# A two-layer transformer block with experts and a state-space scan: scatters that don't wait for each other, and scan inputs made in another order

## The chip, the cores and the metric

The kernel runs on one core of one Trainium2 chip. The metric is device time in microseconds (us), as the median of repeated executions. A core has five engines with their own instruction streams: TensorE (PE in the profile; its weight loads are PEld), VectorE (DVE), ScalarE (ACT), GpSimd (POOL) and SyncE (SP, which here only issues DMAs). They wait for each other by semaphores. TensorE writes to PSUM, a small memory in banks of 128 x 512 float32; all other data lie in SBUF or in the chip's main memory.

## What is computed

Four sequences (B = 4) of 1024 tokens with 128 features pass two layers. Each layer modulates a layer norm by shift and scale, adds a gated mixer, norms again and adds a gated mixture of experts. The mixer of layer 0 is causal attention with 16 heads; that of layer 1 is a selective scan. Cut to what matters:

```python
# layer 0
h = _layernorm(x) * (1 + ca) + sa
x = x + ga * attention(h)                       # 16 heads, causal
h = _layernorm(x) * (1 + cb) + sb
x = x + gb * ffn0(h)     # 8 experts, each token goes to its best 2
# layer 1
x_conv = silu(conv1d(x_main) + conv_b)          # x_main, z = split(h @ W_in)
B_sel, C_sel, delta = ..., ..., softplus(x_conv @ W_xproj[:, -1])
h_t = exp(delta_t * A) * h_(t-1) + delta_t * B_t * u_t      # the scan
y_t = sum_n h_t * C_t
y = (y + x_conv * D_param) * silu(z);  x = x + ga * (y @ W_out)
# then 8 experts again, top 2, with a capacity of tokens for each expert
```

Tokens are sorted to experts by their router's choice. On the chip this is a scatter: each token's normed row (128 float32) is written to a table in main memory at its expert's place, the experts read blocks of rows from the table, write their results to another table, and a gather brings them back.

## The kernel before

**Attention (0 to about 1402 us).** Eight stages, one for each sequence and half of the heads, each with eight blocks of 128 queries in the order 7, 0, 6, 1, 5, 2, 4, 3. A block's scores come from TensorE (`sc`), VectorE adds the mask and finds the maximum (L644), ScalarE exponentiates (L657), POOL divides by the sum (`pr`, L663), TensorE turns the result (`pt`, L672) and multiplies by the values (`po`). POOL also clears a part of the next `pr` (memset, L793) and adds results to `x` (L191).

Beside it, in the stages (1,0), (2,0) and (3,0), runs the **sorting** of the sequence before it (`sort_tokens`, from L364): norm, router, top 2, places, and then 16 scatters (L418), one for each tile of 128 tokens and each choice. The experts of that sequence (`Blocks`) run in the following stage; their first step reads the table (`fxe`, L440).

**The scan stage (1404 to 1848 us).** `scan_inputs(b)` (L923) makes, for one sequence: norm `xn`, turned features `hT`, convolution `p1` and its activation `xc`, `z`'s activation `sz`, `delta` (`pd`, softplus, `dg`), `dt`, `du` = dt*xc (L977, POOL), `bb` and `cc`. Every matmul of it writes to one PSUM bank, tag "m" (bufs = 1), except for sequence 0. `scan` (L988) then runs 32 chunks for each sequence: a product `pu` (TensorE), its multiplication by `bb` (L997, VectorE), `da` (L999, ScalarE), the scan `h` (L1001, VectorE), and `hc` = h*cc (L1005, POOL). `py` collects four `hc` on TensorE, and `scan_output` finishes half a sequence.

The main loop (from L1275) goes over the sequences and, after each pair of chunks, takes a few steps of generators that run beside the scan (`Beside`: from which pair on, how many steps): the inputs of the next sequence, the sort of sequence 3 and its experts, the returns, and the **dispatch** of the sequence before it (L1027: norm, router, places and 16 scatters `slots_in`, L1088, to two tables in turn, one for each choice). The Tile framework schedules the issued instructions onto the engines' queues by its own priorities; every engine then works its queue in order. A scatter is an indirect DMA that POOL issues; a second one into the same table is taken for a write to the same place and waits until the first has landed.

**After the scan.** The last dispatch, the experts of layer 1, eight for each of two choices (1884 to 2006 us), the last half sequence's own table (`g_in`, eight scatters), and the returns.

Of the kernel before, what the change touches and what calls it, by code (L numbers as in the profile page):

```python
# [18 lines left out]
P = 128  # L19
# [30 lines left out]
def adaln_two_layers(ctx: ExitStack, tc: tile.TileContext, I: dict, out: bass.AP):  # L50
# [14 lines left out]
    def load(pool, name, eng=nc.sync):  # L65
# [9 lines left out]

    causal = cst.tile([P, P], F32, name="causal")
    nc.gpsimd.memset(causal, 0.0)
    nc.gpsimd.affine_select(
        out=causal, in_=causal, compare_op=ALU.is_ge, fill=NEG, base=0, pattern=[[-1, P]], channel_multiplier=1
    )  # L80
# [251 lines left out]
    kept, first_made = {}, []  # L332
# [31 lines left out]
    def sort_tokens(b, kept, pool, ps, hpool, tag, xtag="fxn"):  # L364
# [5 lines left out]
        yield from feature_steps(xn, hT, ps, modT[0][:, 4, b : b + 1], modT[0][:, 3, b : b + 1])  # L370
        pl = ps.tile([P, TB, NE], F32, tag="m", name="fpl")
# [8 lines left out]
        pin = ps.tile([P, TB + 1, NE], F32, tag="m", name="fpin")  # L380
        pinf = pin.rearrange("p t e -> p (t e)")
        mm(nc, pinf[:, : TB * NE], before, flat, stop=False)
        for n in range(1, TB):
# [3 lines left out]
        mm(nc, pin[:, TB, :], ones, mine)  # L387
        yield
# [8 lines left out]
        blocks, upto, which = yield from find_blocks(pin[:, TB, :], NB, sm)  # L397
# [7 lines left out]
            pos, upto.unsqueeze(1).to_broadcast([P, TB, NE]), float(P), pin[:, :TB, :], ALU.mult, ALU.add  # L405
# [9 lines left out]
        kept[b] = expert, placei, w  # L415
        for t in range(TB):
            for k in range(2):
                nc.gpsimd.indirect_dma_start(  # L418
                    out=f_in[b][:, :],
                    out_offset=bass.IndirectOffsetOnAxis(ap=placei[:, k, t : t + 1], axis=0),  # L420
                    in_=xn[:, t, :],
                    in_offset=None,
                )
                yield

    class Blocks:
# [9 lines left out]
        def load(self, n):  # L436
            rows_in = f_in[self.b].rearrange("(q p) d -> p q d", p=P)
            m = min(3, NB - 3 * n)
            self.xe = self.pool.tile([P, 3, D], F32, tag="fxe", name="fxe")
            nc.sync.dma_start(self.xe[:, :m], rows_in[:, 3 * n : 3 * n + m])  # L440
# [55 lines left out]
    with ExitStack() as es:  # L496
# [23 lines left out]
        MW = 512 + QG  # L520
        mask = aw.tile([P, MW], F32, name="mask")
# [5 lines left out]
        def zero_steps():  # L527

            for slots in f_in + xd + [g_in]:
                flat = slots.rearrange("(p r) d -> p (r d)", p=P)  # L530
                for at in range(0, flat.shape[1], 512):
                    n = min(512, flat.shape[1] - at)
                    nc.sync.dma_start(flat[:, at : at + n], mask[:, :n])
                    yield
# [234 lines left out]
        zeros, gates = zero_steps(), gate_steps()  # L769
        for at, (b, c) in enumerate(stages):  # L770
# [9 lines left out]
            for n, i in enumerate(order):  # L780
# [13 lines left out]
                for g in range(4):  # L794
# [14 lines left out]
                    if at < 2:  # L809
                        next(zeros, None)  # L810
# [8 lines left out]
            if at == 1:  # L819
                drained(zeros)  # L820
# [32 lines left out]
    with ExitStack() as es:  # L853
# [69 lines left out]
        def scan_inputs(b):  # L923

            def made_of(g, to, w, of):
                bank = ps_m.tile([P, 512], F32, tag=next(tags), name="p1")
                mm(nc, bank, w, of)
                nc.scalar.copy(to[:, half_of(g)], bank)
# [10 lines left out]
            if b == 0:  # L939
                xc, sz, dl = first_made  # L940
                tags = itertools.cycle(("m", "d"))
                dg = spread_delta(dl)

                for g in range(2):
                    tok = half_of(g)
                    made_of(g, dt, ones, dg[g])
                    nc.gpsimd.tensor_mul(du[:, tok], dt[:, tok], xc[:, tok])
                    made_of(g, bb, m_B, xc[:, tok])
                    made_of(g, cc, m_C, xc[:, tok])
                return sz, xc, dt, du, bb, cc  # L950
            tags = itertools.repeat("m")
# [10 lines left out]
            for g in range(2):  # L962
                tok = half_of(g)
                p1 = ps_m.tile([P, 512], F32, tag="m", name="p1")
# [3 lines left out]
                p2 = ps_m.tile([P, 512], F32, tag="m", name="p2")  # L968
                mm(nc, p2, m_in[:, D:], hT[:, tok.start + 3 : tok.stop + 3])
                nc.scalar.activation(sz[:, tok], p2, AF.Silu)  # L970
                yield
            dl = yield from delta_steps(xc, ps_m)
            dg = spread_delta(dl)
            yield
            for g in range(2):
                made_of(g, dt, ones, dg[g])
            nc.gpsimd.tensor_mul(du, dt, xc)  # L977
            yield

            for to, w in ((bb, m_B), (cc, m_C)):  # L980
                for g in range(2):
                    made_of(g, to, w, xc[:, half_of(g)])
                yield
# [118 lines left out]
        def dispatch_last():  # L1102
# [63 lines left out]
            for t in range(nt):  # L1166
                for k in range(2):
                    nc.gpsimd.indirect_dma_start(
                        out=g_in[:, :],
                        out_offset=bass.IndirectOffsetOnAxis(ap=placei[:, k, t : t + 1], axis=0),  # L1170
                        in_=hx[:, t, :],
                        in_offset=None,
                    )
# [7 lines left out]
        sent = []  # L1181

        def last_experts():
# [11 lines left out]
            def rows(q):  # L1195
                n = min(4, nb - q)
                ins[q] = eb.tile([P, 4, D], F32, tag="gxe", name="gxe")
                nc.sync.dma_start(ins[q][:, :n], rows_in[:, q : q + n])
# [76 lines left out]
        for b in range(B):  # L1275
# [3 lines left out]
            if b == 0:  # L1279
                beside.append(Beside(first_returns(B - 2, db, 6), 4, 1))  # L1280
                beside.append(Beside(sort_tokens(B - 1, kept, db, ps_m, db, "hT2", "hx"), 2, 4))
# [7 lines left out]
            if b + 1 < B:  # L1289
                inputs = Beside(scan_inputs(b + 1), 5 if b == 2 else 2, 3 if b == 2 else 2)  # L1290
                beside.append(inputs)
            hcs, late = [], None
# [230 lines left out]
```

## Time and profile before

| what | value |
|---|---|
| three runs | 2079.97, 2082.40 and 2082.79 us; median 2082.4 |
| the profiled execution | 2072.22 us, its span 2070.5 |
| mean granted TensorE clock | 0.923 of full speed |
| attention | 0 to about 1402 us |
| scans, first to last | 1415 to 1848.5 us |
| experts of layer 1 | 1884 to 2006 us |
| a scan `h`, 128 x 512 | 1209 ns, with a carry 1268 (medians) |
| a scatter `blocks_in` on POOL | 982 ns (median of 64), landing 2.3 us after issue |

The page gives each engine's busy time, the span in 40 slices, the groups of instructions by line, and the releasers of idle time. Busy shares over the span hide the stages. So the trace is read by stretches: the busy time of each engine between two moments, beside the granted clock (PEclk). A waits row names who waited, for whom, the total, how often, and the longest. A timeline row has the start, the duration, the engine and line, and in brackets the idle time before it and what ended that.

### The profile page before, as it was taken

How to read it: one execution, taken by the hardware profiler on the slowest of the kernel's cores; microseconds unless marked ns; L12 is line 12 of the kernel's file. 1: busy time of each engine (PE TensorE's matmuls, PEld its weight loads, DVE VectorE, ACT ScalarE, POOL GpSimd, SP SyncE). 2: the span in 40 equal slices, each digit the busy share in tenths (PEclk: the TensorE clock that was granted, in tenths of full speed). 3: DMA queues.
4: the chain of work that ended last, by engine and by line, in shares of the span. 5: the costliest groups of instructions: out<-in, count | busy, mean ns of one | idle time of the engine just before them, and what ended most of it. 6: DMA issues, size and time to landing. Idle time of an engine off the chain costs nothing. (4 is left out here: it accounts for less than half of the span.)

```text
span 2070.5 us, 29042 instructions
## 1 busy us (share of the span) xinstructions
PE 1779.8 (86%) x8957; PEld 964.2 (47%) x8957; DVE 1331.4 (64%) x4005; ACT 944.8 (46%) x2071; POOL 1000.4 (48%) x1282
## 2 busy tenths in 40 slices
PE   5999899898999899899989899997779757757994
PEld 2444454453555345455535445553335423325774
DVE  5666556665667666566766566567858887782144
ACT  2364453743455374355455445455556345422321
POOL 3345335446333634633363653227654775773145
PEclk8899999999999999999999999998879887967997
DMA  6502002002222201212210122111003230002255
GB/s 202 186 1 52 1 1 52 1 26 63 64 64 78 56 1 32 78 54 71 78 40 1 48 68 68 51 43 38 31 27 111 76 108 13 8 20 83 80 156 177
DMA packets 104332, 124.63 MB, mean 60 GB/s; under 512 B 15088, under 2 KB 68720, under 8 KB 104176
## 3 DMA queue, kind: packets, MB, share of 16 engines
q1 hardware_dynamic: 83872, 98.75, 15.9%
q0 software_dynamic: 8192, 16.74, 2.7%
q10 hardware_dynamic: 12112, 7.29, 1.2%
q8 instruction: 71, 1.16, 0.2%
q14 instruction: 85, 0.70, 0.1%
HBM read 68.38 MB, written 33.42 MB: 49 GB/s over the span
## 5 line engine op out<-in xcount | busy, mean ns | idle before, releaser
L663 POOL TENSOR_SCALAR pr<-pr,den 128x32 f32<-128x32 f32 (+31 forms) x512 | 356.2, 711 | 308.2 <-DVE den L660 300.2
L657 ACT ACTIVATE pr<-pr,nb 128x32 f32<-128x32 f32 (+31 forms) x512 | 371.7, 727 | 164.5 <-DVE nb L644 158.5
L672 PE MATMUL pt<-ident,pr 128*128 128x128 f32 x2304 | 342.2, 283 | 47.2 <-POOL pr L663 37.2
L672 PEld LDWEIGHTS pt<-ident,pr 128*128 128x128 f32 x2304 | 253.9, 142 | 242.5 <-POOL pr L663 78.1
L46 PE MATMUL sc<-k,q 64*128 64x512 f32 (+14 forms) x1536 | 333.6, 527 | 33.6 <-DVE nb L644 25.5
L46 PE MATMUL po<-pT,v 128*64 128x512 f32 x1152 | 342.6, 621 | 2.8 <-DVE pT L676 2.8
L674 ACT COPY pT<-pt 128x512 f32<-128x512 f32 x288 | 167.5, 582 | 353.9 <-PE pt L672 302.5
L644 DVE CUSTOM_DVE_ANT_0 pr<-sc,mask 128x512 f32<-128x512 f32 (+15 forms) x512 | 272.8, 559 | 67.4 <-PE sc L46 57.0
L676 DVE COPY pT<-pt 128x512 f32<-128x512 f32 x288 | 198.2, 688 | 159.4 <-PE pt L672 145.9
L46 PEld LDWEIGHTS sc<-k,q 64*128 64x128 f32 x1536 | 125.4, 195 | 186.9 <-DVE nb L644 88.6
L1005 POOL TENSOR_TENSOR hc<-h,cc 128x512 f32<-128x512 f32 x128 | 161.7, 1276 | 87.7 <-DVE h L1001 32.2
L46 PE MATMUL pu<-du,spread 128*128 128x512 f32 x256 | 149.6, 694 | 54.5 <-DVE h L1001 43.5
L793 POOL MEMSET pr<- 128x288 f32 x128 | 42.4, 340 | 245.8 <-PE pt L672 241.6
L644 DVE CUSTOM_DVE_ANT_0 pr<-sc,mask,nb 128x416 f32<-128x416 f32 (+15 forms) x256 | 120.0, 496 | 7.3 <-PE sc L46 6.2
L999 ACT ACTIVATE da<-dt,negA 128x512 f32<-128x512 f32 x128 | 91.4, 718 | 62.7 <-DVE h L1001 62.3
L46 PEld LDWEIGHTS po<-pT,v 128*64 128x64 f32 x1152 | 68.9, 135 | 84.0 <-issue 41.4
L46 PEld LDWEIGHTS pu<-du,spread 128*128 128x128 f32 x256 | 47.6, 213 | 128.4 <-DVE h L1001 74.6
L1391 POOL DMA_INDIRECT y<-slots_out,slot x56 | 56.6, 1010 | 88.4 <-PE ph L46 52.1
L613 POOL TENSOR_TENSOR q<-rot_u,rot_v 128x512 f32<-128x512 f32 x64 | 81.3, 1272 | 36.4 <-DMA rot_v<-rot_w 35.3
L997 DVE TENSOR_TENSOR pu<-pu,bb 128x512 f32<-128x512 f32 x128 | 85.1, 684 | 18.0 <-PE pu L46 9.2
L657 ACT ACTIVATION_READ_ACCUMULATOR pr<-pr,nb 128x1 f32 x512 | 96.2, 188 | 0.0
L418 POOL DMA_INDIRECT blocks_in<-fxn,f_placei x64 | 64.6, 1009 | 57.3 <-DMA blocks_in<-fxn,f_placei 46.6
(281 smaller groups left out, 2695.3 us busy)
## 6 DMA issues: line engine op xcount, KB each, us to landing
fw<-in_f_w SPq DMA_DIRECT2D x92, 320.0 KB, 2.9
rot_v<-rot_w SPq DMA_DIRECT2D x300, 64.0 KB, 2.0
gw<-in_g_w SPq DMA_DIRECT2D x15, 512.0 KB, 5.7
fxe<-blocks_in SPq DMA_DIRECT2D x28, 192.0 KB, 2.5
blocks_out<-fye SPq DMA_DIRECT2D x28, 192.0 KB, 2.8
blocks_in<-mask SPq DMA_DIRECT2D x20, 256.0 KB, 2.9
slots_in<-mask SPq DMA_DIRECT2D x16, 256.0 KB, 3.7
g_w<-in_g_w SPq DMA_DIRECT2D x8, 512.0 KB, 7.3
```

The lines of the kernel that those rows point to most:

```text
L46: return nc.tensor.matmul(out, lhsT, rhs, start=start, stop=stop)
L418: nc.gpsimd.indirect_dma_start(out=f_in[b][:, :], out_offset=bass.IndirectOffsetOnAxis(ap=placei[:, k, t : t + 1], axis=0), in_=xn[:, t, : ...
L613: nc.gpsimd.tensor_add(to, u.rearrange("p (n q) -> p n q", q=QG), v.rearrange("p (n q) -> p n q", q=QG))
L644: nc.vector.tensor_tensor_reduce(out=pr[hp][:, g, lo:hi], in0=sc[:, hp, : hi - lo], in1=mask[:, MW - hi + lo :] if hi == nk else mask[:, : ...
L657: nc.scalar.activation(p, p, AF.Exp, bias=nb[:, last, hp : hp + 1], scale=-1.0, accum_out=den[:, hp : hp + 1])
L663: nc.gpsimd.tensor_scalar(p, p, den[:, hp : hp + 1], 1.0, ALU.mult, ALU.mult)
L672: next_to(hp == 0 and g == 0, lambda: nc.tensor.transpose(to, p, ident))
L674: nc.scalar.copy(pT[:, hp, :], pt)
L676: nc.vector.tensor_copy(pT[:, hp, :], pt)
L997: nc.vector.tensor_mul(pu, pu, bb[:, tok])
L999: nc.scalar.activation(da, dt[:, tok], AF.Exp, scale=negA[:, c : c + 1])
L1005: nc.gpsimd.tensor_mul(hcs[-1], h, cc[:, tok])
```

## The change

Four things, named by their place:

1. Scatters into one table no longer wait for each other. A new helper declares that they write different rows. A scatter now waits only for the clearing of its table, and a read of the table waits for all of its scatters. This holds for `blocks_in` (L418) and `g_in` (L1168), not for `slots_in`.
2. In sequence 0's loop, ten steps each are taken of the sort of sequence 3 and of `scan_inputs(1)`, ahead of the first scan.
3. `scan_inputs` for the sequences 1 to 3 makes `sz` after `delta`'s product, `bb` and `cc` between the steps of softplus, and `dt` and `du` last and in halves. Two PSUM banks take turns ("m" and "g"), except for sequence 2, which keeps one.
4. The sort of sequence 3 uses the PSUM bank "d"; the sort copies its counts from PSUM to SBUF (`ahead`) so that the bank comes free; the mask `causal` lies in a buffer of another pool.

```diff
+    def scatter(group, out, at, in_, fill):
+        ins = nc.gpsimd.indirect_dma_start(
+            out=out, out_offset=bass.IndirectOffsetOnAxis(ap=at, axis=0), in_=in_, in_offset=None
+        ).ins
+        if group:
+            tc.declare_no_dep(ins, group=group[0], reason="different rows")
+        else:
+            group.append(f"rows of {ins.name}")
+        tc.add_to_no_dep_group(group[0], ins)
+        after_all(ins, fill, "zeros")
+        group.append(ins)
+
+    def behind(read, group):
+        after_all(read.ins, group[1:], "scattered rows")
...
+        ahead = sm.tile([P, TB + 1, NE], F32, tag="f_ahead", bufs=1, name="f_ahead")
+        nc.vector.tensor_copy(ahead, pin)
...
-        nc.gpsimd.indirect_dma_start(
-            out=f_in[b][:, :],
...
+                scatter(arrived[b], f_in[b][:, :], placei[:, k, t : t + 1], xn[:, t, :], zeros[b])
...
-            nc.sync.dma_start(self.xe[:, :m], rows_in[:, 3 * n : 3 * n + m])
+            behind(nc.sync.dma_start(self.xe[:, :m], rows_in[:, 3 * n : 3 * n + m]), arrived[self.b])
...
-            tags = itertools.repeat("m")
+            free = b != 2
+            tags = itertools.cycle(((ps_m, "m"), (ps_g, "g"))) if free else itertools.repeat((ps_m, "m"))
...
-                p2 = ps_m.tile([P, 512], F32, tag="m", name="p2")
-                mm(nc, p2, m_in[:, D:], hT[:, tok.start + 3 : tok.stop + 3])
-                nc.scalar.activation(sz[:, tok], p2, AF.Silu)
                 yield
-            dl = yield from delta_steps(xc, ps_m)
-            dg = spread_delta(dl)
-            yield
+            delta = delta_steps(xc, ps_m)
+            next(delta)
             for g in range(2):
+                p2 = new_bank()
+                mm(nc, p2, m_in[:, D:], hT[:, g * 512 + 3 : g * 512 + 515])
+                nc.scalar.activation(sz[:, half_of(g)], p2, AF.Silu)
+            yield
+            try:
+                next(delta)
+                for g in range(2):
+                    made_of(g, bb, m_B, xc[:, half_of(g)])
+                yield
+                next(delta)
+                for g in range(2):
+                    made_of(g, cc, m_C, xc[:, half_of(g)])
+                yield
+                next(delta)
...
+            except StopIteration as end:
+                dg = spread_delta(end.value)
+            yield
+            for g in range(2):
+                tok = half_of(g)
                 made_of(g, dt, ones, dg[g])
-            nc.gpsimd.tensor_mul(du, dt, xc)
-            yield
-
-            for to, w in ((bb, m_B), (cc, m_C)):
-                for g in range(2):
-                    made_of(g, to, w, xc[:, half_of(g)])
-                yield
+                nc.gpsimd.tensor_mul(du[:, tok], dt[:, tok], xc[:, tok])
+            yield
...
-                beside.append(Beside(sort_tokens(B - 1, kept, db, ps_m, db, "hT2", "hx"), 2, 4))
+                beside.append(Beside(sort_tokens(B - 1, kept, db, ps_m, db, "hT2", "hx", "d"), 2, 4))
...
+            if b == 0:
+                for f in (beside[1], inputs):
+                    f.take(10)
```

## The prediction

> **What bounds the kernel now.** First the busy times: no engine is full over the whole span.
>
> ```profile
> PE 1779.8 (86%) x8957; PEld 964.2 (47%) x8957; DVE 1331.4 (64%) x4005; ACT 944.8 (46%) x2071; POOL 1000.4 (48%) x1282
> ```
>
> TensorE leads because attention (until about 1402 us) is its work; the change acts mostly where it does not lead. So the next view is busy time by stretch, cut at the first and last scans `h` of each batch:
>
> ```profile
> core 0: us, PE busy (x) PEld busy (x) DVE busy (x) ACT busy (x) POOL busy (x), PEclk, DMA share, GB/s
> 1415.10:1499.30 84.20, 65.80 (x200) 27.05 (x198) 73.45 (x133) 46.16 (x84) 58.17 (x54) 0.84 0.08 26
> 1499.30:1530.80 31.50, 17.69 (x46) 7.93 (x47) 9.39 (x57) 14.46 (x24) 15.04 (x15) 0.57 0.06 19
> 1530.80:1627.40 96.60, 84.91 (x414) 48.08 (x412) 86.81 (x181) 55.96 (x105) 50.87 (x45) 0.98 0.27 81
> 1627.40:1634.90 7.50, 6.11 (x17) 3.56 (x18) 1.95 (x7) 1.28 (x2) 6.84 (x7) 0.60 0.12 33
> 1634.90:1742.90 108.00, 75.81 (x288) 35.63 (x286) 92.23 (x184) 48.12 (x92) 76.18 (x64) 0.83 0.22 75
> 1742.90:1771.00 28.10, 17.40 (x70) 10.08 (x71) 10.90 (x53) 14.03 (x25) 21.70 (x19) 0.74 0.11 33
> 1771.00:1848.50 77.50, 54.60 (x164) 18.47 (x162) 73.87 (x116) 30.34 (x59) 57.54 (x48) 0.83 0.04 12
> 1848.50:1884.20 35.70, 13.18 (x52) 9.63 (x52) 21.49 (x85) 5.63 (x10) 20.09 (x19) 0.50 0.20 58
> ```
>
> Rows 1, 3, 5 and 7 are the four scan batches: VectorE is busy 85 to 95% of them and sets their length. Rows 2, 4 and 6 are stretches in which no scan runs: VectorE idles 22.1, 5.5 and 17.2 us there (length less its busy column). Those 44.8 us are what earlier inputs can win; the last row is the wait from the last scan to the experts.
>
> Third, what attention loses to scatters: POOL issues them, and each waits until the one before it has landed. The waits by engine have it (us in total, times, longest):
>
> ```profile
> POOL blocks_in L418 <- DMA blocks_in<-fxn,f_placei: 46.6, 35, 3.4
> ```
>
> 46.6 us of POOL waiting, 8.9 of it in the scan stage. Attention pays only where TensorE runs dry behind it; the timeline at 480 us is such a place:
>
> ```profile
> 481.74 0.98 POOL L418 DMA_INDIRECT blocks_in<-fxn,f_placei  x1 [3.20 <-DMA blocks_in<-fxn,f_placei]
> 484.26 0.97 POOL L418 DMA_INDIRECT blocks_in<-fxn,f_placei  x1 [1.54 <-DMA blocks_in<-fxn,f_placei]
> 485.25 1.27 POOL L608 TENSOR_TENSOR k<-rot_u,rot_v 128x512 f32<-128x512 f32 x1
> 486.49 1.52 POOL L663 TENSOR_SCALAR pr<-pr,den 128x608 f32<-128x608 f32 x2
> 487.31 0.18 PEld L672 LDWEIGHTS pt<-ident,pr 128*128 128x128 f32 x1 [7.68 <-POOL pr L663]
> ```
>
> Two chained scatters hold POOL, `pr` comes late, and TensorE starts its transposes 7.7 us late.
>
> **Part 1, unchained scatters in attention (three stages of 16).** Before, one takes 0.98 us plus 1.54 us of waiting, 2.5 us from start to start. The nearest row without a chain is `slots_in` (two tables in turn): starts at 1763.01, 1764.30 and 1765.59, 1.28 us. A table's 16 then hold POOL 20.5 us in place of some 40. But unchained they are also grouped otherwise: in the changed program's order on POOL they stand in runs of 2, 3, 1 and 10 in the first two stages, and 2, 5, 3, 1 and 5 in the third. A run of ten is 12.8 us; behind it on POOL wait the memset of the next `pr`, an add to `x`, and the normalisation of `pr`, for which TensorE waits. I followed the first stage: one `pr` comes 2.6 us later (TensorE loses some 2), the run of ten holds up a memset that VectorE's reduction needs (a new hole of about 3.5), and then POOL is free of scatters and the hole before 487.31 nearly goes (7.5 us, with what follows). Net gain 3 to 4 us; the second stage likewise 2 to 3; in the third a new 3 us stands against 4 us of idling at 1185 to 1189, net 2. I take **8 us of gain**. Ends: the three holes cost with their cold matmuls about 11, 9 and 13 us; losing 5 of them to nothing leaves 28 as the best; 5 us of loss, if the third hole stays in each stage beside the new one, less what TensorE catches up, is the worst I count.
>
> The change also adds waits: the tables' reads (`fxe`, on SyncE, with the weight loads `fw` queued behind) wait for all 16 scatters, and the scatters for the clearing of their table. The read waited for the last of the chain already, and the clearing ended stages earlier: 0, and if the last of the sixteen lands 2 us late, 2.
>
> The matmul clock weighs on this: it was granted at 0.50 from 484 to 492 us, behind the 7.5 us hole, but 1.00 between 1152 and 1155 us, in a 3.0 us hole, and 0.58 in the next 3. [...] The 64 scatters here beside busy VectorE took 966 to 1212 ns, median 982; the sum goes by these rows.
>
> **Part 2, inputs of batch 1 (gap of 31.5 us).** The chain there: last products of conv, `p`, `sz`, `pd` until 1511.9, softplus until 1518.4 shared with a norm, `dg` 1518.72, two matmuls of 2.06 with copies of 0.59 each (cold, clock 0.57), `du` in one piece from 1525.49 (2.35), `pu`, and
>
> ```profile
> 1530.08 0.70 DVE L997 TENSOR_TENSOR pu<-pu,bb 128x512 f32<-128x512 f32 x1 [8.59 <-ACT xn L168]
> ```
>
> The step that is late is the chain's start: the norm of batch 1 falls late in batch 0, its PSUM comes from one bank, and POOL alternates products `hc` with chained scatters (2.5 us each) until 1504. In the changed order the ten early steps of norm and features, two banks and free scatters put both halves of `du` behind `hc` 16 and 18 of 32, so the inputs are ready half a batch ahead. The gap's 9.4 us of VectorE work moves into batch 0, whose own idle is 10.8 us. Idle removed: 22.1 at best; I take **18**, because what is left of batch 0's chain (`hc`, `py`) must still end. Lower end 5, if batch 0 grows by most of it.
>
> **Part 3, what that costs at the head.** Two norms go ahead of the first scans' partners on ScalarE: 16 normalisations at 0.39 (five took 1.94) are 6.2 us, and three to four table loads of 1.28, part of which stand there already (1414 to 1422). Scans wait for `da` on ScalarE meanwhile. Total 6 to 11 us on ScalarE, covered by two or three scans in flight: I take **7 us of loss**, bounds 0 and 12.
>
> **Part 4, inputs of batches 2 and 3.** Halved `du` and the `dt` products: the first half's scan no longer waits for the second matmul and copy (2.1 + 0.6) and half of `du` (1.2): 3.9 us. Gap of 7.5: **3** (0 to 5.5). In the gap of 28.1 also the `du` at 1766.56 stood behind three scatters (1763.01 to 1766.56, 3.6 us), where now `slots_in` come earlier, between `hc` 88 and 96; and `sz` comes after `pd` (2 us). 3.9 + 3.6 + 2 = 9.5: **10** (4 to 17.2). What is late next is softplus, a chain of small VectorE operations.
>
> **Part 5, the tail.** Dispatch of batch 2, which used the last gap, now runs inside batch 3 and later: after the last `hc` stand 16 `slots_in` scatters where 8 stood. 8 × 1.28 = 10 us, partly beside the norm of the last rows: **6 us of loss** (0 to 10). The eight `g_in` scatters come back to back, but the first experts cover them: 0 (0 to 5 of gain). Four copies `f_ahead` of about 0.2 us: **1 of loss**. The mask `causal` in another buffer and the sort's own bank: 0; the sort's matmuls lie beside scans, and were the cover gone, a product waiting for bank "d" would cost about one 2 us step, which is inside the bounds.
>
> **Sum.** 8 + 18 − 7 + 3 + 10 − 6 − 1 = 25 us. The profiled execution took 2072.2 (span 2070.5 and 1.7 around it), so 2047 by its scale. It lies 10.2 below the median of the runs shown (2082.4); I forecast that median's successor, 2082.4 − 25 = **2057**. All good ends together would be 28 + 22 + 0 + 5.5 + 17 + 0 + 5 = 78, all bad ones −5 + 5 − 12 + 0 + 4 − 10 − 1 = −19; neither set is likely whole.
>
> **Rivals.**
> *Everything closes* (15%): attention's holes and all three gaps go, the tail stays covered. 28 + 22 − 7 + 5 + 14 − 6 = 56, so 2026. For it: VectorE's idle in the gaps is no work of any engine's own, the clock in the first gap is 0.57. Against: runs of ten on POOL.
> *VectorE and the tail take it back* (17%): batches 0 and 3 grow by most of what the gaps lose. Then 5 from part 2, 5 from part 4, 8 from attention, less 7 and 3: 8, so 2074. For it: VectorE is 95% busy in batch 3, so what moves there lengthens it.
> *It doesn't do what it says* (6%): the queue still takes one scatter of a table at a time, and 2.5 us stay from start to start. Then attention gives 0, part 2 its lower 5, part 4 3 and 4, less 7, 3 and 1: 1, so 2081, no measurable change. Against: two tables in turn did run at 1.28.
> *Slower, by runs of scatters on POOL* (12%). In attention TensorE stayed fed 3.3 us after its last `pr` (476.6 to 479.87). A run of ten holds POOL for 12.8, so 9.5 may be bare, and with 8 us at half clock as at 484 some 4 more: 13.5 in two stages, 3 in each of two runs of five in the third, 33 in all, if the old holes stay as well. With 17 left from the scan stage that is 16 slower, 2098. It decides where attention loses more than 17 us. Against: after the run POOL has no scatter left, and the old holes should go.
>
> **Numbers.** My own case, 2045 to 2069, 50%. Faster by over 0.2% (4 us, about what a measurement can tell from none): 50 + 15 + 17 = 82%; same 6%; slower 12%. The range 2024 to 2086 leaves out half of the first rival and the most of the last, some 17%.
>
> **What would show it.** Scatters of one table 1.28 us apart in all stages; no `pt` waiting 7 us for `pr` near 487, but a wait of about 3.5 for VectorE near 473 to 477; the next batch's first `h` within 10 us of the last at 1500, and 18 us in place of 28 before batch 3; batch 0 some 7 to 15 us longer; the tail about 41 us. It is wrong if batch 0 grows by over 20 us, or if attention ends later than before.

## The result, and the profile after

The changed kernel takes 2093.2 us (median of 5 runs, 2087.0 to 2095.8), the kernel before 2082.8 beside it (5 runs, 2080.0 to 2086.1): a ratio of 1.0041, 95% interval 1.0022 to 1.0060. It is slower by 0.2 to 0.6%, where 25 us of gain were forecast. A second measurement (e5 below) gave 1.0021 (1.0005 to 1.0037). A ratio here comes from runs made in turn, so the quotient of two medians can differ from it a little.

The profiled execution after has a span of 2085.2 us, clock 0.927. First the busy times from the page of the changed kernel:

```profile
PE 1776.4 (85%) x8957; PEld 959.8 (46%) x8957; DVE 1339.4 (64%) x4009; ACT 942.1 (45%) x2069; POOL 1002.8 (48%) x1285
```

Nearly nothing moves in them: VectorE has 8 us more with four instructions more. So again the stretches, cut at the first and last scan `h` of each batch (1.1 us lie between batches 0 and 1 now, and batches 1 and 2 touch):

```profile
core 0: us, PE busy (x) PEld busy (x) DVE busy (x) ACT busy (x) POOL busy (x), PEclk, DMA share, GB/s
1421.00:1527.30 106.30, 82.59 (x252) 36.07 (x250) 82.83 (x144) 53.36 (x98) 73.78 (x73) 0.81 0.10 31
1527.30:1528.40 1.10, 1.10 (x4) 0.56 (x4) 1.10 (x3) 0.72 (x1) 1.10 (x2) 1.00 0.00 0
1528.40:1649.30 120.90, 99.94 (x487) 59.20 (x486) 108.03 (x256) 63.46 (x123) 67.43 (x56) 0.93 0.29 84
1649.30:1753.50 104.20, 72.89 (x250) 29.75 (x248) 91.08 (x186) 50.33 (x92) 75.47 (x65) 0.83 0.16 59
1753.50:1767.80 14.30, 7.99 (x21) 3.27 (x22) 4.02 (x7) 3.13 (x5) 10.39 (x9) 0.58 0.06 23
1767.80:1846.80 79.00, 55.28 (x186) 20.66 (x184) 72.58 (x129) 35.43 (x69) 54.23 (x43) 0.87 0.01 6
1846.80:1886.20 39.40, 13.35 (x52) 9.69 (x52) 21.33 (x92) 7.14 (x12) 27.21 (x26) 0.51 0.16 56
```

The gaps did close: 31.5 to 1.1, 7.5 to 0, 28.1 to 14.3 us, 51.7 in all. But batch 0 grew from 84.2 to 106.3 and batch 1 from 96.6 to 120.9. From the first scan to the last row's end it is 469.1 before, 465.2 after. VectorE's columns split these 4 us exactly. It idles 34.5 us less in the gaps (44.8 to 10.3), 16 more inside the batches (39.9 to 55.9), 4 more in the last row, and it is busy 10.9 more (370.1 to 381.0) for the work it had before.

In attention the chain of scatters is gone. Of the waits on POOL this row takes the place of the 46.6 us on DMA, of which 0.2 are left; "issue" is the 0.3 us between two instructions:

```profile
POOL blocks_in L338 <- issue: 15.4, 56, 0.3
```

The place that the forecast showed at 480 us is clean: the same `pr` (128x608) runs without a scatter ahead of it, and the weight load of the transposes behind it, which waited 7.7 us, follows without idle time. These are rows of the changed kernel's timeline:

```profile
490.17 1.53 POOL L689 TENSOR_SCALAR pr<-pr,den 128x608 f32<-128x608 f32 x2 [0.80 <-DVE den L686]
...
491.20 0.31 PEld L698 LDWEIGHTS pt<-ident,pr 128*128 128x128 f32 x3
```

But they come 3.9 us later in the execution than before (487.31). Behind the run of ten scatters, 463.5 to 476.0, TensorE now idles 2.7 us before 474.4 and 2.0 before 479.5.

And yet attention ends no earlier: the first scan starts at 1421.0, before at 1415.1.

Last, 12.7 us of the 14.7 between the two spans lie behind the scan stage: the end part, from the experts' first matmul to the end, is 186.3 before and 199.0 after. e1, e5 and e13 to e18 show that this is not the change.

### The profile page after: what moved, and what is told of

Its sections match the earlier page's. It is cut to its first block, busy times and chain, and to the rows that moved or that the text cites. A ratio compares the mean times of both kernels' runs of the same rounds, so it can differ in the third digit from the quotient of the medians.

```text
span 2085.2 us, 29078 instructions
## 1 busy us (share of the span) xinstructions
PE 1776.4 (85%) x8957; PEld 959.8 (46%) x8957; DVE 1339.4 (64%) x4009; ACT 942.1 (45%) x2069; POOL 1002.8 (48%) x1285
## 5 line engine op out<-in xcount | busy, mean ns | idle before, releaser
L698 PE MATMUL pt<-ident,pr 128*128 128x128 f32 x2304 | 346.8, 285 | 51.8 <-POOL pr L689 29.2
L46 PE MATMUL po<-pT,v 128*64 128x512 f32 x1152 | 347.8, 626 | 3.0 <-DVE pT L702 1.9
L46 PEld LDWEIGHTS pf<-fxT,fw 128*128 128x128 f32 x552 | 70.5, 194 | 41.0 <-DVE fye L502 14.4
```

The lines of the kernel that those rows point to most:

```text
L46: return nc.tensor.matmul(out, lhsT, rhs, start=start, stop=stop)
L698: next_to(hp == 0 and g == 0, lambda: nc.tensor.transpose(to, p, ident))
```

## Experiments

After the two traces I held that the gain was lost in three places: a new hole in attention's third sorting stage, batches that grow because VectorE's small operations are drawn out beside POOL (50 us in the scan stage after, 43 before), and the tail. The rivals were that the order itself (engines' queues, not POOL's reads) lengthens the batches, that runs of scatters on POOL cost it, and that the tail's 13 us have nothing to do with the program. Ratios are against the kernel before, run beside them on the same chip, with 95% intervals.

### The 13 us at the end

**e1: the kernel before again.** No edit.

> The kernel before once more, unchanged, for a second trace of it. From the first matmul of layer 1's experts to the end of the span it took 186.3 us in the first trace (1884.2 to 2070.5), and the changed kernel 199.0 (1886.2 to 2085.2), with a stretch around 2028 to 2034 us in which TensorE, ScalarE, VectorE and SyncE all stand still. Theory: such a stall can fall on any execution, whichever kernel; then this trace may show some 190 to 200 too, and first scan, last scan and gaps as before (1415, 1848, 31.5 and 28 us). Rival: the stall comes with the change; then 186 again within 2.

Measured: 2074.1 us, end part 186.2.

**e5: the changed kernel again.** No edit.

> The changed kernel once more, unchanged, beside the others on one chip, for a second trace. Theory: the 13 us that its first trace lost behind the start of layer 1's experts (199.0 us to the end of the span, against 185 to 186 in the five other traces) is a stall of that execution and not of the program: 185 to 187 now, first scan at 1421, start of the experts at 1886, and 0 to 0.2% slower than before. Rival: the stall belongs to the program: 199 again and 0.4% or more slower.

Measured: 2072.3 against 2070.1, ratio 1.0021 (1.0005 to 1.0037). Span 2071.8, end part 185.3. So the same program had 199.0 in one trace and 185.3 in another, and the span of e1 (2072.3) is within 0.5 us of that of e5. In e13 to e18, on two other chips where the kernel before has a median of 2081, the end part is 198 to 199 us in versions of both kernels (e13: 198.5; e18: 199.2). It goes with the chip, as far as these traces tell, and not with the program. That would also explain why the profiled execution of before lay 10 us under its median. Why the end part differs was not found.

### Attention: who else waits for the scatters

The third sorting stage has a new hole. The timeline of the changed kernel shows it, with the rows of `pt`, of the scatters and of ScalarE:

```profile
1167.09 1.09 PE L698 MATMUL pt<-ident,pr 128*128 128x128 f32 x8
...
1169.14 0.97 POOL L338 DMA_INDIRECT blocks_in<-fxn,f_placei  x1 [0.30 <-issue]
1170.41 0.97 POOL L338 DMA_INDIRECT blocks_in<-fxn,f_placei  x1 [0.30 <-issue]
...
1172.96 0.97 POOL L338 DMA_INDIRECT blocks_in<-fxn,f_placei  x1 [0.30 <-issue]
1175.30 0.49 ACT L162 ACTIVATE fxn<-x,ln_away,ln_r 128x128 f32<-128x128 f32 x1 [8.92 <-DMA blocks_in<-fxn,f_placei]
1175.70 0.56 ACT L700 COPY pT<-pt 128x512 f32<-128x512 f32 x1
...
1176.32 1.97 PE L698 MATMUL pt<-ident,pr 128*128 128x128 f32 x8 [7.12 <-ACT pT L700]
```

Read it from below. TensorE waits 7.1 us for a copy `pT`. The copy stands on ScalarE behind a normalisation that writes `fxn`, and this one waited 8.9 us until the last scatter, which reads `fxn`, had landed. It is the first norm of layer 1 (L740), whose result shares the one buffer "fxn" with the sort's. Before, this norm started at 1196.4 us, after the last scatter, and waited for nothing; with free scatters the scheduler puts it ahead of the copies. The scatters themselves run 1.28 us apart, as forecast.

To compare stages, a measure that does not hang on one hole: the time on POOL from one pair of `pr` memsets to the seventh pair after it, at the same places in each of the three stages (in the third, 1130 to 1268 us before). It is listed for all 20 traces:

| scatters in attention | stage 1, median | stage 2, median | stage 3, range |
|---|---|---|---|
| chained (6 traces) | 138.3 | 140.2 | 138.8 to 143.0 |
| free, buffer shared (7) | 136.3 | 136.7 | 145.5 to 147.6 |
| free, own buffer (7) | 136.4 | 137.9 | 136.6 to 140.1 |

Stage 3 tells the second row from the others: nothing of it comes below 145.5, nothing of theirs above 143.0. In stages 1 and 2 the single values overlap (135.1 to 141.8 chained, 133.9 to 143.3 free), and the two profiled executions have 141.1 and 140.2 before, 141.3 and 140.9 after. So a gain there is likely by the medians, but not shown.

**e6: only attention's scatters chained again.**

```diff
-                scatter(arrived[b], f_in[b][:, :], placei[:, k, t : t + 1], xn[:, t, :], zeros[b])
+                scatter(arrived[b], f_in[b][:, :], placei[:, k, t : t + 1], xn[:, t, :], zeros[b], chained=b < B - 1)
```

> The changed kernel, where only the scatters of attention (sequences 0 to 2) wait for each other again; those of sequence 3 and of g_in stay free. Theory: the first scan comes back to 1414 to 1416 (1421 in the changed kernel), the scan stage stays at 465 us from first scan to experts (469 before), so 5 us faster than the changed kernel and 3 to 5 faster than before. Rival: attention's scatters are neutral and the first scan falls later for another reason (the order of loads, the mask's buffer): first scan at 1420 or later.

Measured: 2068.0, ratio 0.9989 (0.9972 to 1.0006); first scan at 1419.4, stage 3 143.0. The first scan's moment varies by up to 13 us between executions of one attention program on different chips (1404.0, 1416.8 and 1412.3 in e12, e15 and e16), so it tells little; stage 3 tells more.

**e10: the kernel before, with free scatters in attention and for `g_in` only.** As the diff's helper, but the scatters of sequence 3 stay chained.

> The kernel before, with free scatters in attention and for g_in only; sequence 3's, beside the first scans, still wait for each other. Theory: of the 24 us that free scatters cost by themselves, 3 to 5 lie in attention, and the rest comes from one run of scatters in batch 0 that holds POOL 20 us while the scans wait for hc; so this one is 2 to 6 us slower than before, with a scan stage of 469. Rival: the loss is spread; 10 us or more slower.

Measured: 2071.3, ratio 1.0014 (0.9998 to 1.0031). Free scatters alone gain nothing; stage 3 has 145.5, with holes of 6.7 us at 1156 and 5.3 at 1174.

**e9: the changed kernel, and layer 1's first norm in another buffer, which is not in use then.**

```diff
-            xn = ab.tile([P, TB, D], F32, tag="fxn", bufs=1, name="fxn")
+            xn = keep.tile([P, TB, D], F32, tag="even0", bufs=1, name="ixn")
```

> The changed kernel, with the normed rows of layer 1's first inputs in another buffer than the one that the third sort's scatters read. Theory: in the changed kernel these normalisations stand in ScalarE's queue ahead of the copies pT and wait 8.5 us for the last scatter to land (TensorE idle 6.7 us at 1171 us), which is the 5 to 8 us that the third sorting stage loses; with a buffer of their own that hole goes, the stage gets 5 us back, and the time is 4 to 7 below the changed kernel. Rival: POOL's run of five scatters ahead of them is the loss; then TensorE still idles 5 us or more there and the time is unchanged.

Measured: 2061.5 against 2069.5, ratio 0.9963 (0.9944 to 0.9981). The timeline of e9 at the place of the hole:

```profile
1165.67 1.09 PE L698 MATMUL pt<-ident,pr 128*128 128x128 f32 x8
...
1169.07 1.09 PE L698 MATMUL pt<-ident,pr 128*128 128x128 f32 x8
...
1172.21 1.09 PE L698 MATMUL pt<-ident,pr 128*128 128x128 f32 x8
```

The same transposes at the same place follow without a wait, beside scatters at 1163.8 to 1169.0 us, 1.28 us apart at the end. With the table's third row, in seven traces, this shows that the shared buffer was the cause of the hole in stage 3. The time of e9 was measured on one chip only.

**e11, and e18 again: e10 with the same buffer edit.**

> The same, with a buffer of its own for layer 1's first inputs. Theory: attention then keeps the gains of its first two sorting stages (3 to 4 us each) without the loss of the third: 3 to 7 us faster than before. Rival: no faster than before, since another wait takes the place of that one in the third stage.

> The kernel before with free scatters in attention and the buffer of its own, nothing changed in the scan stage, again. Theory: 0.3 to 0.5% faster than before, as the first time (0.37%), scan stage 469. Rival: within 0.2% of before.

Measured: e11 2060.5 against 2069.5, 0.9963 (0.9944 to 0.9982); e18 on another chip 2074.1 against 2081.1, 0.9966 (0.9949 to 0.9982). Free scatters are worth 7 to 9 us as soon as nobody waits for their source. Found on two chips, this version is faster than the kernel before, and it needs nothing of the new order of inputs. On the chip of e11 its gain lies in attention: the first scan starts at 1402.9, with chained scatters at 1416.0 and 1414.2 (e1, e3). In e18 it starts at 1410.4, in e13 and e14, chained and on another chip, at 1411.7; where the 7 us of e18 lie is not shown.

### The scan stage: order, early steps, POOL

**e2: the kernel before, all scatters of `blocks_in` and `g_in` free.** The scatter parts of the diff, and nothing else.

> The kernel before with one part of the change only: scatters of one table don't wait for each other. Theory, from the two traces: in attention the scatters' runs on POOL cost about as much as the chain did, and 6 to 7 us more in the third sorting stage, so the first scan falls some 6 us later (1421); in the scan stage the free scatters bring the first gap (31.5 us) down by up to 10. Together -5 to +5 us against before. Rival (my prediction): attention gains 8, the gap 10: 15 us or more faster.

Measured: 2091.8 against 2066.5, ratio 1.0116 (1.0096 to 1.0136), 485.0 us of scan stage. That missed what I expected. In batch 0 all 16 scatters of the last sort came in one run of 20 us; the timeline of e2 shows its end:

```profile
1506.82 0.97 POOL L344 DMA_INDIRECT blocks_in<-fxn,f_placei  x1 [0.30 <-issue]
1507.81 6.15 POOL L1029 TENSOR_TENSOR hc<-h,cc 128x512 f32<-128x512 f32 x5
1509.12 3.71 DVE L1025 TENSOR_TENSOR_SCAN h<-da,carry,pu 128x512 f32<-128x512 f32 x3 [12.83 <-POOL hc L1029]
```

The products `hc` of three finished scans wait behind the run, and as `h` has three buffers, the next scan waits 12.8 us until the first product has freed one. This is the mechanism of the forecast's slower rival, but in the scan stage and not in attention. It explains the growth of batch 0 (96.0 in place of 84.2); batch 1 grows as well (115.3 in place of 96.6), and that was not followed. In the changed kernel the same 16 scatters stand in runs of 3, 3, 5 and 5 with `hc` between them. The wait is shorter there, but it is there; behind the last run, which ends at 1501.0 us, and a `du`:

```profile
1502.27 2.48 POOL L1049 TENSOR_TENSOR hc<-h,cc 128x512 f32<-128x512 f32 x2
1503.57 1.28 DVE L1045 TENSOR_TENSOR_SCAN h<-da,carry,pu 128x512 f32<-128x512 f32 x1 [6.38 <-POOL hc L1049]
```

In batch 0 the scans wait 7.0 us for `hc` in all in after, e5 and e9, and 3.1 in the kernel before.

**e3: the changed kernel with all scatters chained.** The helper keeps only its scatter.

```diff
-        if group:
-            tc.declare_no_dep(ins, group=group[0], reason="different rows")
-        else:
-            group.append(f"rows of {ins.name}")
-        tc.add_to_no_dep_group(group[0], ins)
-        after_all(ins, fill, "zeros")
-        group.append(ins)
...
-        after_all(read.ins, group[1:], "scattered rows")
+        return read
```

> The changed kernel, only that scatters of one table wait for each other as before. Theory: attention gets its 6 us back (first scan at 1415), while batch 0's chain of inputs is somewhat later; about 2 to 8 us faster than the changed kernel, near the kernel before. Rival: the free scatters are what closes the first gap; then the gap comes back by 10 us or more, and the time is 5 to 15 above the changed kernel.

Measured: 2069.6, ratio 1.0010 (0.9996 to 1.0024); scan stage 470.5, with batch 0 at 100.4, batch 1 at 128.2 and batch 2 at 115.2. In batch 0 the scans wait 0.4 us for `hc`, and it is 6 us shorter than with free scatters (106.2 to 106.5 in after, e5 and e9); so by this trace, runs of scatters on POOL cost some 6 us in batch 0. Batches 1 and 2 take back what that saves. So within the change, too, free scatters bring nothing that can be told from noise (e5: 1.0005 to 1.0037).

**e4: the changed kernel without the early steps of sort and inputs.**

```diff
-                for f in (beside[1], inputs):
-                    f.take(10)
+                pass
```

> The changed kernel without the ten early steps of the two norms. Theory: VectorE's idle time in batch 0 (23.5 us in the changed kernel, 10.7 before) falls back by about 8, but the inputs of batch 1 come later and a gap of 5 to 15 us opens: within 5 us of the changed kernel. Rival: the early norms are the loss; then 8 to 12 us faster than the changed kernel, level with before.

Measured: 2067.8, ratio 0.9998 (0.9982 to 1.0014); scan stage 466.5, batch 0 103.0, first gap 1.1. The first gap closes without the early steps.

**e14: neither free scatters nor early steps, only the rest (the edits of e3 and e4 together).**

> The changed kernel without the early steps and with scatters that wait for each other: of the change only the order of the inputs, their two banks, halved du and the sort's bank are left. Theory: these alone close the first gap (below 10 us from 31.5) and lengthen batch 0 (84 before, 103 without early steps, 100 with chained scatters) to 96 to 102; the scan stage stays within 3 us of 469. Rival: the free scatters or the early steps are needed for the gap; then 15 us or more of it stay, and batch 0 is below 92.

Measured: 2097.6 us in a single run, beside 2081.3 for the kernel before; scan stage 486.5: the first gap 0.7, but batch 2 128.5 in place of 108.0. The order alone closes the first gap, and then costs 20 us in batch 2, which I had not expected.

**e7: `pu` issued one pair of chunks ahead.** In batch 0 after, one pause between two scans is 13.6 us long. The timeline of TensorE there:

```profile
1461.30 0.43 PE L46 MATMUL fpin<-f_both,before 128*128 128x64 f32 x2 [2.39 <-DVE f_both L399]
...
1464.87 2.05 PE L46 MATMUL p<-hT,conv_in 128*128 128x512 f32 x2
1466.71 1.71 PE L46 MATMUL pd<-m_dt_sb,xc 128*128 128x1 f32 x8
1468.28 2.05 PE L46 MATMUL pu<-du,spread 128*128 128x512 f32 x2
```

The sort's counts `fpin` wait for VectorE and stand ahead of `p`, `pd` and the `pu` that the next scan needs. That scan starts at 1471.21; the one before it started at 1456.42. The edit issues the pair's `pu` before the scan of the pair ahead of it.

```diff
+            pus = products(*pair_of(0), *scanned)
...
-                hcs += scan([4 * (2 * n % 4 + r) + n // 2 for r in range(2)], g, carry, *scanned)
+                hcs += scan(pair_of(m)[0], g, pus, carry, *scanned)
+                if m + 1 < NCH:
+                    pus = products(*pair_of(m + 1), *scanned)
```

> The changed kernel, with the products pu of each pair of chunks issued one pair ahead, before the steps that are taken beside the scan. Theory: batch 0 is long (106 us, with a hole of 14.8 at 1456) because TensorE's queue holds the sort's and the inputs' products ahead of the next pu, and each of them waits for a chain on other engines; then the hole falls below 9, batch 0 to some 98, and the time 5 to 10 below the changed kernel. Rival: pu can't be earlier, since its bank is only free after the scan two pairs back, or batch 0 is long by its work on VectorE alone: within 3 us of the changed kernel.

Measured: 2069.9, ratio 1.0001 (0.9983 to 1.0018); batch 0 110 us, and the pause stays (15.4 from scan to scan). The timeline of e7 shows that `pu` did move:

```profile
1457.37 0.62 PE L46 MATMUL fpin<-f_both,before 128*128 128x64 f32 x2 [3.65 <-DVE f_both L399]
...
1461.16 2.06 PE L46 MATMUL pu<-du,spread 128*128 128x512 f32 x2
...
1466.46 0.17 DVE L266 COPY sp_r<-pd 128x8 f32<-128x8 f32 x1 [2.26 <-PE pd L46]
...
1467.16 1.22 DVE L1050 TENSOR_TENSOR_SCAN h<-da,pu 128x512 f32<-128x512 f32 x1
```

It now runs directly behind the counts and ahead of `pd`. But the counts wait for VectorE as before, and the scan then stands on VectorE behind a copy of `pd`, for which VectorE waits. So the wait only moved to another queue. That the order of work on TensorE and VectorE makes this pause is read from the two timelines; no run here removes it.

**e8 and e13: `hc` without its reads, after and before.** Two memsets stand in for the product and write the same tile; the product h*cc is left out, and with it the true y. Two memsets take 1.0 us (in a row, a pair starts every 0.93) and the product 1.27, so POOL is also less busy: 265.4 in place of 309.6 us of the scan stage after, 267.2 in place of 306.4 before.

```diff
-                nc.gpsimd.tensor_mul(hcs[-1], h, cc[:, tok])
+                nc.gpsimd.memset(hcs[-1], 0.5)
+                nc.gpsimd.memset(hcs[-1], 0.25)
```

> The changed kernel with POOL's product hc = h * cc left out: two memsets of the same tile stand for it, which write as much and read nothing, so the scan's output isn't formed from h. Theory: VectorE's small operations are drawn out while POOL reads two inputs (49 us in all of them together in the scan stage of the changed kernel, 41 before, measured as duration over the shortest of the same form); without POOL's reads they fall to their shortest, the sum below 15 us. Rival: they are long for a reason of their own (the wait for other engines counted in): the sum stays above 35.

> The kernel before with POOL's product hc = h * cc left out and two memsets in its place, as in the run of the changed kernel with them (scan stage there 426 us, from first scan to experts; 465 to 470 with the product). The product itself makes 469 against 465 to 470. Theory A: the drawn-out small operations of VectorE eat what the closed gaps give; without POOL's reads the change's gain in the scan stage shows, so this run's scan stage is 436 or more, 10 or more above the changed kernel's. Theory B: the gain is eaten by the order on TensorE and ScalarE; then 424 to 431.

The question comes from rows like these, VectorE's norm of eight numbers per partition in the changed kernel, and POOL's products beside them:

```profile
1426.63 1.28 POOL L977 TENSOR_TENSOR du<-dt,xc 128x512 f32<-128x512 f32 x1
1426.70 1.25 DVE L148 TENSOR_TENSOR ln_r<-ln_r 128x8 f32<-128x8 f32 x1 [2.81 <-ACT ln_r L144]
...
1429.00 2.61 DVE L150 TENSOR_SCALAR ln_r<-ln_r 128x8 f32<-128x8 f32 x1
1429.06 2.51 POOL L1049 TENSOR_TENSOR hc<-h,cc 128x512 f32<-128x512 f32 x2
```

In the kernel before, the same two steps of a norm ran in the gap, beside a scatter on POOL that starts at 1517.24 and takes 0.97 us:

```profile
1517.47 0.17 DVE L154 TENSOR_TENSOR ln_r<-ln_r 128x8 f32<-128x8 f32 x1 [1.33 <-ACT ln_r L150]
...
1517.92 0.26 DVE L156 TENSOR_SCALAR ln_r<-ln_r 128x8 f32<-128x8 f32 x1
```

0.17 and 0.26 us become 1.25 and 2.61, the length of the POOL products beside them. Over the scan stage, VectorE's operations (the scans and `pu` aside) take longer than the shortest of the same line and shape. Where such stretches overlap they count once, and so they add up to 43 us before and 45 in e1, and to 50, 52 and 50 in after, e5 and e9; 39 to 48 of these us belong to operations beside a POOL tensor operation. The two windows, each from the first scan to the experts' first matmul, are e8 (after):

```profile
1418.48:1844.45 425.97, 318.67 (x1243) 157.19 (x1241) 350.27 (x810) 214.67 (x399) 265.43 (x390) 0.85 0.17 53
```

and e13 (before):

```profile
1411.65:1849.06 437.41, 319.64 (x1245) 155.01 (x1243) 357.67 (x809) 211.46 (x397) 267.20 (x389) 0.85 0.17 52
```

With the memsets, the new order has 11.4 us less scan stage than the old (437.4 to 426.0). With the products it has 465.2, 470.1 and 469.3 (after, e5, e9) against 469.1 and 470.1 (before, e1), one or two us less on the mean. So with the products, some 10 us of what the new order saves is taken back. The sum above falls to 28 (e8) and 31 (e13), not below the 15 I expected: it was some 6 us longer in the new order and is 3 us shorter now, a turn about as large as the 10. So the drawn-out operations fit, as was expected ahead of e13. They are not shown to be the cause alone: there is one trace of each, on two chips, and POOL is some 40 us less busy in both, which other waits may profit from. What is left of the sum lies mostly beside POOL operations, memsets too; one 128x8 `ln_r` of the form that took 0.26 took 6.42 us at 1665 in e8, beside seven pairs of memsets in a row. So a memset is no clean absence of POOL.

### Put together

**e12, and e16 again: e9 without the early steps.**

> The changed kernel without the ten early steps and with the buffer of its own: what the experiments so far would put together. Theory: first scan 4 to 6 us earlier than in the run without the early steps (1419), scan stage 466 to 469: 4 to 8 us faster than before. Rival: level with before within 2 us.

> The same kernel as the one 0.46% faster than before (no early steps, buffer of its own, free scatters everywhere), again. Theory: the gain is the program's: 0.3 to 0.6% faster than before again, scan stage 466 within 2. Rival: it was the chip: within 0.2% of before.

Measured: e12 2058.9 against 2069.5, 0.9954 (0.9936 to 0.9973); e16 on another chip 2077.3 against 2081.1, 0.9993 (0.9976 to 1.0009). The first gain did not come again.

**e15, and e17 again: free scatters in attention with their own buffer, the new order, no early steps, chained scatters beside the scans.** It was to join the parts that had helped.

> Free scatters in attention and for g_in, the buffer of its own for layer 1's first inputs, the changed order of inputs, no early steps, and chained scatters beside the scans. Theory: first scan at 1403 to 1405, the scan stage 2 to 5 below the 466 of the run with free scatters there, if POOL's runs of scatters cost in batch 0: 10 to 14 us faster than before. Rival: chained scatters there cost as much as runs; then level with the last run, 9 us faster than before.

> The same with chained scatters beside the scans, again. Theory: the scan stage (476 against 466) is the program's, the first scan's 13 us are the execution's: 8 to 12 us slower than the kernel beside it. Rival: both are the program's: 20 us or more slower than the kernel beside it; or neither: level.

Measured: 2095.6 against 2081.3, 1.0064 (1.0040 to 1.0088), and 2094.5 against 2081.1, 1.0072 (1.0047 to 1.0097); scan stage 476, batch 2 127 us. Both say that it is slower, as in e14 (a single run): with the new order, without early steps and with chained scatters batch 2 is 20 us longer, and attention's gain is lost again. What in batch 2 is late there stays open. The parts don't add up one by one: to free the scatters beside the scans lengthens the scan stage by 18 us in the old order (e10 466.9, e2 485.0) and shortens it by 10 in the new one without early steps (e15 476.2, e12 466.2).

## Why the prediction was wrong

**What bounds it: right.** VectorE set the length of the batches, the gaps were its idle time, and the three holes behind chained scatters were real: the one before 487 us is gone, scatters start 1.28 us apart, no `pt` waits 7 us for `pr` there. The hole expected near 473 to 477 is there too: 2.7 us before 474.4, with a second of 2.0 behind it.

**Part 1, 8 us of gain: wrong in the third stage.** Stages 1 and 2 gain 2 and 3.5 us by the medians above, against 3 to 4 and 2 to 3, though the values overlap. The third was to gain 2 and loses 7. The step that failed is the one on the waits that the change adds, put at 0: it counted who waits to read the table and who clears it, and not who waits to overwrite the rows that the scatters read. That dependency existed before, too; it cost nothing because the norm stood later in ScalarE's order. The price was a run of scatters that must land, on an engine with the critical copy queued behind. Not all 64 scatters of the kernel before ran beside busy VectorE: in 16 it did nothing (median 996 ns), in 29 it was busy for over half of the time (median 1014 ns). With its own buffer the part is worth 9 and 7 us (e11, e18), against the 8; that this meets the 8 is partly luck, as the medians of the three stages give 4 to 5.

**Parts 2 and 3, 18 us from the first gap less 7 for batch 0: near in the net, wrong in each.** The gap gave 30.4. Batch 0 grew 22.1, and the forecast's own mark for being wrong was 20; the other mark, attention ending later, came true as well. The net is 8.3 against 11. Of batch 0's growth, VectorE's busy time is 9.4 and its idle 12.7. "The gap's 9.4 us of VectorE work moves into batch 0, whose own idle is 10.8 us" is the sentence that failed. Of the gap's 57 VectorE instructions the 18 of softplus and `dg` moved there, and they take 7.4 us (durations added) where they took 3.8 in the gap. Idle in batch 0 did not fill up but went to 23.5: moved work brings its waits along. Part 3 looked for the cost on ScalarE. Runs of free scatters on POOL cost some 6 us there (e3 is without them); part lies in VectorE's small operations beside POOL (supported by e8 and e13), and part in the order on TensorE and VectorE (read from the timelines, not shown).

**Part 4, 3 and 10 us: right in its place, and the price was missing.** The gaps gave 7.5 and 13.8, more than forecast. But batch 1, for which the forecast's sum has no term, grew by 24.3: VectorE has 75 instructions and 21.2 us more there. The step that failed is this missing term: the rest of the first gap's work went to batch 1 and not to batch 0. Batch 1 has 52 instructions of norms (`ln_`), 16 us with their durations added, where it had none before; the first gap had 36 of them and has none now. VectorE was 90% busy in that batch already, so what moves there lengthens it. The forecast says this of batch 3, in a rival, and not of batch 1. Batches 2 and 3 changed by -3.8 and +1.5. So part 4 gave nothing in place of 13.

**Part 5, 6 us at the tail: right in sign.** 35.7 became 39.4, a loss of 3.7. All twelve traces with the new order and the products have 39.3 to 39.7, the six others 35.5 to 35.9.

**The sum.** Parts 2 to 5 were to give 17 us and gave 4, 0 and 0 (after, e5, e9). By the stages' medians attention gives -1 to -2 in place of 8. That makes about nothing in place of 25, against 8.5 and 4 us slower by the two ratios. The traces are single executions, and these spread by more than the rest (the kernel before had 2058.8 to 2075.5 in 29 runs on one chip); where the rest lies stays open.

**The rivals.** "VectorE and the tail take it back" is what the scan stage did, though in batches 0 and 1 and not 0 and 3; with attention's 8 it still ended faster. "Runs of scatters on POOL" had the right sign. Its mechanism appears beside the scans, with a wait of 12.8 us in e2 and of 6.4 in the changed kernel; in attention it cost 2.7 and 2.0 us near 480.

**The 10 us** by which the profiled execution lay under the median were carried through the forecast as an offset. The end parts of 185 and 199 us would account for them: where the kernel before has a median of 2066 to 2070 us the end part is the short one, where it has 2081 the long one.

## What to carry to other kernels

When a dependency is taken away, the scheduler moves more than the freed instructions: look for everyone who shares a buffer with them, writers above all, and for what is queued behind those on their engine. Idle time of the bounding engine in a gap is not free room elsewhere: work moved into a busy stretch lengthens it and brings its own waits (here batch 1, in which VectorE was 90% busy, grew by 24.3 us), so price the stretch that receives it, not only the gap that loses it. And try the smallest part of a change by itself: here one part of four, with one buffer more, was worth 7 to 9 us, and the rest nothing that lasted.

## What the runs showed of the hardware

In the profile after, two VectorE operations of 128x8 numbers lasted as long as the POOL products beside them: 1.25 us beside a `du` of 1.28, and 2.61 beside two `hc` of 2.51. In the profile before, the same two steps took 0.17 and 0.26 beside a scatter of 0.97. In e8 one of the second form took 6.42 beside seven pairs of memsets. Over the scan stage, what VectorE's operations take beyond the shortest of their line and shape adds up to 43 to 52 us in before, e1, after, e5 and e9, one tenth of it; 39 to 48 of them belong to operations beside a POOL tensor operation.

The end part takes 185 to 186 us in all traces from chips 3 and 8 (e1 186.2, e5 185.3) and 198 to 199 in all from chips 10 and 11 (e18 199.2, e13 198.5). The profile before has the short one, 186.3, and the profile after the long one, 199.0. In the profile after, TensorE, ScalarE, VectorE and SyncE stand still together three times for 2 us or more ahead of a last stretch of 5.5: 4.3 us from 2030.2, 3.1 from 2044.4 and 2.0 from 2057.2. In the profile before they do so only in the last stretch, for 6.2 us from 2052.0.
